# A transformer layer's experts with their weights copied into a new layout beside attention, and used as the stationary side of the first product

## The chip, the cores and the metric

The kernel runs on one core of a Trainium2 chip, as one launch. The metric is the time of the device in microseconds (us), the median over several runs. A profile is one more execution, recorded by the hardware profiler. The core has a matrix engine (PE, with a weight load, PEld, ahead of each matmul), a vector engine (DVE), a scalar engine for activations (ACT), GpSimd (POOL), and SyncE (SP), which mostly issues transfers. Sixteen DMA engines move data between the DRAM and the on-chip SBUF; PSUM is the on-chip memory of eight banks that PE writes its results into.

## The reference

Two layers on 4096 tokens (2 x 2048) of 512 features, all in float32. The first is a linear attention, the second a mixture of experts; each is normalised before and after and added to its input.

```python
x = x + _layernorm(_L0_attn_ref(_layernorm(x), Wq, bq, Wk, bk, Wv, bv, Wo))
x = x + _layernorm(_L0_ffn_ref(_layernorm(x), wg, w1, v1, w2))

# attention: 16 heads of 128, 4 key/value heads
sq, sk = elu(q) + 1, elu(k) + 1
kv = einsum('bhsd,bhse->bhde', sk, v)
attn = einsum('bhsd,bhde->bhse', sq, kv) / (einsum('bhsd,bhd->bhs', sq, sk.sum(axis=2))[..., None] + EPS)

# experts: 32 of them, 8 per token, F = 192 hidden features
weights, idx = top_k(softmax(x @ wg.T), 8); weights = weights / weights.sum()
h  = silu(ragged_dot(xs, w1, group_sizes)) * ragged_dot(xs, v1, group_sizes)   # xs: tokens sorted by expert
ys = ragged_dot(h, w2, group_sizes)
out = zeros.at[t_s].add(ys * w_s[:, None])
```

## The kernel before

**Attention.** `keys_of` normalises and transposes all tiles of one of the two sequences and forms the keys' state; `finish_kv` and `fold_wo` turn it into one matrix per head. Then four blocks of 512 tokens for each sequence, eight in all, go through `attn_block`. It walks over 16 heads: `stage_q(h)` forms the head's queries on PE (L552, eight instruction records: four chunks of 128 input features, two records per float32 matmul), ACT takes Relu and Exp (L555, L556) and DVE forms `sq` (L559). After every fourth head `stage_n` forms the normalisers on PE (L567), DVE takes the reciprocal (L571), and they go through DRAM: SP writes `nr_d` (L573) and loads it back four times, spread over all partitions, as `nb` (L576), with which DVE multiplies `sq` (L579). Eight heads later `stage_o` multiplies with the head's matrix (L584). While a block runs, the four tiles of 128 tokens of the block before are finished (`finish_tile`): added to the input, normalised, written to `xn_d`, and routed. `route_tile` finds the eight experts of each token and scatters token numbers and weights into a list per expert, with eight indirect DMAs per tile on POOL (L203). In the first block SP also clears the accumulators in DRAM (`acc_d`, L429).

**Experts.** The lists are cut into blocks of 128 tokens of one expert each; two halves of them ("sides", s = 0 and 1) are worked on in pairs. 138 pairs run: 24 in a first round, planned from the first six attention blocks, and 114 in a second one, of which the last ten stand behind conditions (`tc.If`) that ask whether there are still pairs to do. For one pair:

- `prepare`: for each side SP reads the expert's number from the plan and loads its weights into one of NR = 3 buffers: `w1t` (L674, [128, 4 x 384]: for each of the four chunks of 128 input features the 192 gate and then the 192 up columns) and `w2t` in two pieces of 128 and 64 rows (L675, L676). A load is skipped where the buffer still holds that expert. POOL gathers the 128 tokens from `xn_d` (L679), PE transposes them in four pieces (`px`, L685), DVE copies them to `xgT` (L687).
- `run_pair`: for each side PE forms `pgu` = tokens x weights (L698): the tokens' transposes are stationary, 384 weight columns move, four chunks, thus eight records; the result has tokens in the partitions and 384 features along the row. ACT takes SiLU of the 192 gate columns (`hs`, L701) and DVE multiplies by the 192 up columns into `hh` (L702), with the features put in an order in which the two sides' 2 x 192 make three pieces of 128. PE transposes the three pieces (`ph`, L710), DVE copies them (`hT`, L712). The second product (`py`, L715 for the first 128 features of a side, L719 for the other 64) gives 512 columns per side; ACT scales by the token's weight (`ysb`, L723) and POOL adds the rows into `acc_d` by an indirect DMA (L724).

PSUM is full in this stage: two banks each for `xt`, `gu` and `y`, one for `ht`, one for the routing.

A scheduler orders the instructions on each engine after the whole program is written; on SP the order inside the expert stage is that of the program text. `tc.issue_after(ins)` keeps what is written under it behind `ins` on that engine. At the end `acc_d` is read back, normalised, added and written out (L767 to L789).

Of the kernel before, what the change touches and what calls it, by code (L numbers as in the profile page):

```python
# [8 lines left out]
F32 = mybir.dt.float32  # L9
I32 = mybir.dt.int32  # L10
U32 = mybir.dt.uint32
AF = mybir.ActivationFunctionType
# [5 lines left out]
P = 128  # L18
# [5 lines left out]
def linear_attention_then_moe(  # L24
# [15 lines left out]
    nc = tc.nc  # L40

    NT, HID = x.shape
    B = 2
# [5 lines left out]
    C = HID // P  # L49
    E = wgT.shape[1]  # L50
    K = 8
    F2 = wgu.shape[1] // C
    F = F2 // 2
    FC = w2r.shape[1] // HID
    FR = F - P
# [4 lines left out]
    NBLK = S // TB  # L60
# [20 lines left out]
    dram = ctx.enter_context(tc.tile_pool(name="dram", bufs=1, space=DRAM))  # L81
# [4 lines left out]

    nr_d = dram.tile([B * NBLK, KVH, GR * TB], F32, name="nr_d")
    list_d = dram.tile([E * CAP + BS, 2], F32, name="list_d")


    const = ctx.enter_context(tc.tile_pool(name="const", bufs=1))
    ident = const.tile([P, P], F32, name="ident")
# [284 lines left out]
    with ExitStack() as actx:  # L377
# [153 lines left out]
        def fold_wo(acc):  # L531
# [9 lines left out]
                ms.append(m)  # L541
            return ms

        def attn_block(b, t, xlT, ksum, ms):

            pa = [ps_acc.tile([P, HID], F32, tag="acc", name=f"acc{s}") for s in range(NS)]
            sq, sqn = {}, {}

            def stage_q(h):
                pq = ps_mm.tile([P, TB], F32, tag="mm", name="pq")  # L550
                for c in range(C):
                    nc.tensor.matmul(pq, wq_sb[:, c, h * P : (h + 1) * P], xlT[:, c, :],  # L552
                                     start=(c == 0), stop=(c == C - 1))
                qe = wk2.tile([P, TB], F32, tag="qe", name="qe")
                nc.scalar.activation(qe, pq, AF.Relu, bias=nbq_sb[:, h : h + 1], scale=-1.0)  # L555
                ex = nc.scalar.activation(qe, qe, AF.Exp, scale=-1.0)  # L556

                sq[h] = sqp.tile([P, TB], F32, tag="sq", name="sq")
                nc.vector.scalar_tensor_tensor(sq[h], pq, bq1_sb[:, h : h + 1], qe, ALU.add, ALU.max)  # L559
                return ex.ins  # L560

            def stage_n(g):

                pn = ps_mm.tile([P, TB], F32, tag="mm", name="pn")
                w = P // GR
                for j in range(GR):
                    nc.tensor.matmul(pn[j * w : (j + 1) * w, :], ksum[:, g, 1, :w], sq[g * GR + j],  # L567
                                     start=True, stop=True)
                nr = wk2.tile([P, TB], F32, tag="tmp", name="nr")
                nc.vector.tensor_scalar_add(nr, pn, NORM_EPS)  # L570
                nc.vector.reciprocal(nr, nr)  # L571
                rows = nr_d[b * NBLK + t, g : g + 1, :]
                nc.sync.dma_start(rows.rearrange("o (j f) -> (o j) f", j=GR), nr[::w, :])  # L573
                for j in range(GR):
                    nb = nbp.tile([P, TB], F32, tag="nb", name="nb")
                    nc.sync.dma_start(nb, rows[:, j * TB : (j + 1) * TB].to_broadcast([P, TB]))  # L576
                    h = g * GR + j
                    sqn[h] = sq.pop(h)
                    nc.vector.tensor_mul(sqn[h], sqn[h], nb)  # L579

            def stage_o(h):
                a = sqn.pop(h)
                for s in range(NS):
                    nc.tensor.matmul(pa[s], a[:, s * P : (s + 1) * P], ms[h],  # L584
                                     start=(h == 0), stop=(h == H - 1))

            for h in range(H + 2 * GR):
                if h < H:
                    ex = stage_q(h)
                if h == H // 2:  # L590
                    mid = ex
                if h < H and h % GR == GR - 1:
                    stage_n(h // GR)
                if h >= 2 * GR:
                    stage_o(h - 2 * GR)
                if h % GR == GR - 1:
                    finish_next()

            for s in range(NS):
                mv, rs = ln_stats(sm, pa[s])  # L600
                x1 = x1p.tile([P, HID], F32, tag="x1", name="x1")
                nc.vector.tensor_scalar(x1, pa[s], mv[:, 0:1], rs, ALU.subtract, ALU.mult)
                waiting.append(((b * S + t * TB) // P + s, x1))
            return mid
# [42 lines left out]
    with ExitStack() as mctx:  # L647
# [5 lines left out]
        hp = pairs.enter_context(tc.tile_pool(name="hp", bufs=3))  # L653
        ps_a = pairs.enter_context(tc.tile_pool(name="ps_a", bufs=2, space=PSUM))
# [4 lines left out]

        w1b = weights([P, C * F2], "w1t")  # L660
        w2b = weights([P, 2, HID], "w2t")

        w2v = w2r.rearrange("r (c h) -> (r c) h", c=FC)
        pairs.enter_context(tc.manual_schedule(engines={mybir.EngineType.SP}))

        def prepare(r, cols, tid, wt, load, xsrc):

            xgTs = []
            for s, c0 in enumerate(cols):
                w1t, w2t = w1b[s][r], w2b[s][r]  # L670
                ld = nc.sync.value_load(load[:, c0 : c0 + 1], min_val=0, max_val=2 * E - 1)
                ex = ld & (E - 1)
                skip = {"cond": ld < E, "bounds_check": "skip_entire_dma"}
                nc.sync.dma_start(w1t, wgu[bass.ds(ex * P, P), :], **skip)  # L674
                nc.sync.dma_start(w2t[:, 0, :], w2v[bass.ds(ex * F + s * FR, P), :], **skip)  # L675
                nc.sync.dma_start(w2t[s * FR : (s + 1) * FR, 1, :],  # L676
                                  w2v[bass.ds(ex * F + (1 - s) * P, FR), :], **skip)
                xg = xg_p.tile([P, HID], F32, tag="xg", name="xg")
                nc.gpsimd.indirect_dma_start(  # L679
                    out=xg, out_offset=None, in_=xsrc,  # L680
# [9 lines left out]

        def run_pair(r, cols, tid, wt, load, xgTs):

            hh = hp.tile([P, 2, F], F32, tag="hh", name="hh")
            for s, xgT in enumerate(xgTs):
                w1t = w1b[s][r]
                pgu = ps_a.tile([P, F2], F32, tag="gu", name="pgu")
                for c in range(C):
                    nc.tensor.matmul(pgu, xgT[:, c, :], w1t[:, c * F2 : (c + 1) * F2],  # L698
                                     start=(c == 0), stop=(c == C - 1))
                hs = hp.tile([P, F], F32, tag="hs", name="hs")  # L700
                nc.scalar.activation(hs, pgu[:, :F], AF.Silu)  # L701
                nc.vector.tensor_mul(  # L702
                    hh[:, s, :].rearrange("p (k c) -> p c k", c=FC),
                    hs.rearrange("p (c k) -> p c k", c=FC),
                    pgu[:, F:].rearrange("p (c k) -> p c k", c=FC),
                )
            hf = hh.rearrange("p s f -> p (s f)")
            ph = ps_a.tile([P, 3, P], F32, tag="ht", name="ph", bufs=1)
            for c in range(3):
                nc.tensor.transpose(ph[:, c, :], hf[:, c * P : (c + 1) * P], ident)  # L710
            hT = hp.tile([P, 3, P], F32, tag="hT", name="hT")
            nc.vector.tensor_copy(hT, ph)  # L712
            py = [ps_a.tile([P, HID], F32, tag="y", name=f"py{s}") for s in range(2)]
            for s in range(2):
                nc.tensor.matmul(py[s], hT[:, 2 * s, :], w2b[s][r][:, 0, :],  # L715
# [114 lines left out]
```

## Time and profile before

| | |
|---|---|
| Median of 3 runs | 2855.16 us (2854.49 to 2856.72) |
| The profiled execution | 2861.29 us, span of its instructions 2859.5 us |
| PE busy | 2645.8 us, 93% of the span, 8443 records |
| DVE, ACT, POOL busy | 37%, 24%, 37% |
| pgu (L698) | 2208 records, 780.0 us busy |
| ph (L710) | 414 records, 100.5 us busy |
| px (L685) | 1104 records, 174.2 us busy |
| hh (L702), hT (L712) | 276 of 355 ns, 138 of 557 ns |
| w1t loads (L674) | 276 issues of 768 KB, a part of them skipped |
| DMA | 399.83 MB, 140 GB/s on average |

A line of the profile names the source line, the engine, the operation, what it writes and reads, and the shapes; "x" is the number of records. Ends of matmuls are modelled and overlap the next one's start, so the time of a run of matmuls is read from start to start. The "idle before" of an instruction names what ended the wait. From the start to about 150 us come the first sequence's keys, then its four attention blocks to about 660, the second sequence's keys to about 820 and its blocks to 1335; the experts follow to 2775, the last normalisation to 2859.

### The profile page before, as it was taken

How to read it: one execution, taken by the hardware profiler on the slowest of the kernel's cores; microseconds unless marked ns; L12 is line 12 of the kernel's file. 1: busy time of each engine (PE TensorE's matmuls, PEld its weight loads, DVE VectorE, ACT ScalarE, POOL GpSimd, SP SyncE). 2: the span in 40 equal slices, each digit the busy share in tenths (PEclk: the TensorE clock that was granted, in tenths of full speed). 3: DMA queues.
4: the chain of work that ended last, by engine and by line, in shares of the span. 5: the costliest groups of instructions: out<-in, count | busy, mean ns of one | idle time of the engine just before them, and what ended most of it. 6: DMA issues, size and time to landing. Idle time of an engine off the chain costs nothing. (4 is left out here: it accounts for less than half of the span.)

```text
span 2859.5 us, 29618 instructions
## 1 busy us (share of the span) xinstructions
PE 2645.8 (93%) x8443; PEld 1310.7 (46%) x8443; DVE 1061.4 (37%) x2432; ACT 674.8 (24%) x1208; POOL 1059.9 (37%) x891
## 2 busy tenths in 40 slices
PE   8999999998999999998779899999999999999850
PEld 3434444444444444444435455555555555555420
DVE  5334544546533536554412222222222222222217
ACT  4332222213331313221211112121212121212114
POOL 1100223122320122223455555555555555554426
PEclk9999999999999999999889999999999999999985
DMA  3291211212111212123647899989787988685548
GB/s 112 86 329 51 68 52 52 68 52 67 37 56 45 71 34 71 53 71 114 161 102 175 212 268 257 274 200 254 165 214 160 314 194 199 137 194 114 104 87 323
DMA packets 179290, 399.83 MB, mean 140 GB/s; under 512 B 29413, under 2 KB 30438, under 8 KB 178610
## 3 DMA queue, kind: packets, MB, share of 16 engines
q0 software_dynamic: 70144, 145.31, 25.1%
q1 hardware_dynamic: 101602, 237.55, 24.9%
q10 hardware_dynamic: 7376, 15.02, 1.4%
q8 instruction: 70, 1.15, 0.2%
q14 instruction: 98, 0.80, 0.1%
HBM read 488.74 MB, written 116.66 MB: 212 GB/s over the span
## 5 line engine op out<-in xcount | busy, mean ns | idle before, releaser
L698 PE MATMUL pgu<-w1t,xgT 128*128 128x384 f32 x2208 | 780.0, 496 | 3.5 <-issue 2.4
L724 POOL DMA_INDIRECT acc_d<-ysb,tid x276 | 441.9, 1601 | 503.8 <-ACT ysb L723 389.5
L203 POOL DMA_INDIRECT list_d<-tw,pi x256 | 252.2, 985 | 979.6 <-DVE pi L201 556.2
L698 PEld LDWEIGHTS pgu<-w1t,xgT 128*128 128x128 f32 x2208 | 399.5, 191 | 327.2 <-issue 109.3
L552 PE MATMUL pq<-xlT,wq_sb 128*128 128x512 f32 x1024 | 463.1, 598 | 1.2 <-DVE sq L559 1.2
L584 PE MATMUL acc<-m,sq 128*128 128x512 f32 x1024 | 463.0, 597 | 0.0
L702 DVE TENSOR_TENSOR hh<-hs,pgu 128x192 f32<-128x192 f32 x276 | 97.3, 355 | 975.9 <-ACT hs L701 838.2
L723 ACT ACTIVATE ysb<-py,wt 128x512 f32<-128x512 f32 x276 | 176.5, 684 | 783.4 <-PE py L719 731.8
L679 POOL DMA_INDIRECT xg<-xn_d,tid x276 | 274.9, 996 | 119.0 <-PE px L685 64.0
L552 PEld LDWEIGHTS pq<-xlT,wq_sb 128*128 128x128 f32 x1024 | 190.7, 190 | 241.5 <-issue 230.8
L584 PEld LDWEIGHTS acc<-m,sq 128*128 128x128 f32 x1024 | 189.1, 190 | 239.6 <-issue 239.1
L715 PE MATMUL py<-w2t,hT 128*128 128x512 f32 x552 | 266.4, 605 | 2.1 <-issue 2.1
L555 ACT ACTIVATE qe<-pq,nbq_sb 128x512 f32<-128x512 f32 x128 | 87.8, 686 | 514.6 <-PE pq L552 509.0
L687 DVE COPY xgT<-px 128x512 f32<-128x512 f32 x276 | 188.3, 683 | 43.6 <-PE px L685 41.3
L559 DVE SCALAR_TENSOR_TENSOR sq<-pq,bq_sb,qe 128x512 f32<-128x512 f32 x128 | 95.8, 748 | 286.0 <-ACT qe L556 285.9
L685 PE MATMUL px<-ident,xg 128*128 128x128 f32 x1104 | 174.2, 284 | 29.1 <-DMA xg<-xn_d,tid 26.7
L701 ACT ACTIVATE hs<-pgu 128x192 f32<-128x192 f32 x276 | 90.3, 330 | 363.2 <-PE pgu L698 336.7
L685 PEld LDWEIGHTS px<-ident,xg 128*128 128x128 f32 x1104 | 135.9, 147 | 56.9 <-issue 32.0
L715 PEld LDWEIGHTS py<-w2t,hT 128*128 128x128 f32 x552 | 107.5, 196 | 109.2 <-issue 74.0
L719 PE MATMUL py<-w2t,hT 64*128 64x512 f32 x552 | 157.1, 642 | 0.0
L710 PE MATMUL ph<-ident,hh 128*128 128x128 f32 x414 | 100.5, 298 | 51.3 <-DVE hh L702 51.2
L469 PE MATMUL pk<-wk_sb,xlT 128*128 128x512 f32 x256 | 119.7, 607 | 0.0
(185 smaller groups left out, 1844.8 us busy)
## 6 DMA issues: line engine op xcount, KB each, us to landing
w1t<-in_wgu_dram SPq DMA_DIRECT2D x276, 768.0 KB
w2t<-in_w2r_dram SPq DMA_DIRECT2D x276, 256.0 KB
w2t<-in_w2r_dram SPq DMA_DIRECT2D x276, 128.0 KB
nb<-nr_d SPq DMA_DIRECT2D x128, 256.0 KB
acc_d<-zero SPq DMA_DIRECT2D x6, 2048.0 KB
xb<-in_x_dram SPq DMA_DIRECT2D x32, 256.0 KB
xr<-in_x_dram SPq DMA_DIRECT2D x32, 256.0 KB
wo<-in_woT_dram SPq DMA_DIRECT2D x32, 256.0 KB
```

The source lines that it names most:

```text
L203: nc.gpsimd.indirect_dma_start(out=list_d[:, :], out_offset=bass.IndirectOffsetOnAxis(ap=pi[:, k : k + 1], axis=0), in_=tw[:, k, :], in_of ...
L469: nc.tensor.matmul(pk, xlT[:, c, :], wk_sb[:, c, :], start=(c == 0), stop=(c == C - 1))
L552: nc.tensor.matmul(pq, wq_sb[:, c, h * P : (h + 1) * P], xlT[:, c, :], start=(c == 0), stop=(c == C - 1))
L584: nc.tensor.matmul(pa[s], a[:, s * P : (s + 1) * P], ms[h], start=(h == 0), stop=(h == H - 1))
L679: nc.gpsimd.indirect_dma_start(out=xg, out_offset=None, in_=xsrc, in_offset=bass.IndirectOffsetOnAxis(ap=tid[:, c0 : c0 + 1], axis=0),)
L685: nc.tensor.transpose(px[:, c, :], xg[:, c * P : (c + 1) * P], ident)
L687: nc.vector.tensor_copy(xgT, px)
L698: nc.tensor.matmul(pgu, xgT[:, c, :], w1t[:, c * F2 : (c + 1) * F2], start=(c == 0), stop=(c == C - 1))
L715: nc.tensor.matmul(py[s], hT[:, 2 * s, :], w2b[s][r][:, 0, :], start=True, stop=False)
L719: mm = nc.tensor.matmul(py[s], hT[rows, 1, :], w2b[s][r][rows, 1, :], start=False, stop=True)
L723: nc.scalar.activation(ysb, py[s], AF.Copy, scale=wt[:, c0 : c0 + 1])
L724: sc = nc.gpsimd.indirect_dma_start(out=acc_d[s][:, :], out_offset=bass.IndirectOffsetOnAxis(ap=tid[:, c0 : c0 + 1], axis=0), in_=ysb, in_ ...
```

## The change

Two new tensors in DRAM, `w1_d` and `w2_d`, hold the experts' weights in a new order: for each chunk of input features the 384 columns stand as the 192 gate columns (0 to 191), then the last 64 up columns (192 to 255), then the first 128 up columns (256 to 383). Read in three strips of 128: gate 0 to 127; gate 128 to 191 with up 128 to 191; up 0 to 127. `w2_d` has the 192 rows of an expert in their plain order.

`lay_out_experts(i)` yields five copies from DRAM to DRAM for four experts: three for `w1_d` (pieces of 768, 256 and 512 bytes) and two for `w2_d` (rows of 2 KB). `attn_block` issues them on ACT's queue after the Exp of heads 1, 4, 7, 10 and 13; with eight blocks this covers the 32 experts with 40 copies, 37.7 MB read and as much written.

`prepare` loads from `w1_d` and `w2_d`. In `run_pair` the weights are now the stationary side: for each side three strips by four chunks, each a matmul of a 128x128 piece of weights with the 128 tokens moving. The result has features in the partitions and tokens along the row, as the second product needs it, so the three transposes and the copy to `hT` are gone. ACT takes SiLU over the first two strips (256 columns), and DVE forms `hT` with two products, one of 128 partitions and one of 64, the latter with operands from different partitions. `pgu` has three buffers, and the bank of `ph` is free for the third.

```diff
--- before.py
+++ after.py
@@ -86,6 +86,10 @@
 
     nr_d = dram.tile([B * NBLK, KVH, GR * TB], F32, name="nr_d")
     list_d = dram.tile([E * CAP + BS, 2], F32, name="list_d")
+
+
+    w1_d = dram.tile([E * P, C * F2], F32, name="w1_d")
+    w2_d = dram.tile([E * F, HID], F32, name="w2_d")
 
 
     const = ctx.enter_context(tc.tile_pool(name="const", bufs=1))
@@ -541,10 +545,26 @@
                 ms.append(m)
             return ms
 
+        def lay_out_experts(i):
+
+            n = E // (B * NBLK)
+            rows = slice(i * n * P, (i + 1) * n * P)
+            src = wgu[rows, :].rearrange("r (c f) -> r c f", c=C)
+            dst = w1_d[rows, :].rearrange("r (c f) -> r c f", c=C)
+            yield lambda: nc.scalar.dma_start(dst[:, :, :F], src[:, :, :F])
+            yield lambda: nc.scalar.dma_start(dst[:, :, F : F + FR], src[:, :, F + P :])
+            yield lambda: nc.scalar.dma_start(dst[:, :, F + FR :], src[:, :, F : F + P])
+            w2s = w2r[i * n * (F // FC) : (i + 1) * n * (F // FC), :]
+            w2x = w2_d[i * n * F : (i + 1) * n * F, :].rearrange("(e c p) h -> c e p h", e=n, c=FC)
+            for c in range(FC):
+                yield lambda c=c: nc.scalar.dma_start(
+                    w2x[c], w2s[:, c * HID : (c + 1) * HID].rearrange("(e p) h -> e p h", e=n))
+
         def attn_block(b, t, xlT, ksum, ms):
 
             pa = [ps_acc.tile([P, HID], F32, tag="acc", name=f"acc{s}") for s in range(NS)]
             sq, sqn = {}, {}
+            moves = lay_out_experts(b * NBLK + t)
 
             def stage_q(h):
                 pq = ps_mm.tile([P, TB], F32, tag="mm", name="pq")
@@ -587,6 +607,9 @@
             for h in range(H + 2 * GR):
                 if h < H:
                     ex = stage_q(h)
+                    if h % 3 == 1 and h < 15:
+                        with tc.issue_after(ex):
+                            next(moves)()
                 if h == H // 2:
                     mid = ex
                 if h < H and h % GR == GR - 1:
@@ -659,8 +682,6 @@
 
         w1b = weights([P, C * F2], "w1t")
         w2b = weights([P, 2, HID], "w2t")
-
-        w2v = w2r.rearrange("r (c h) -> (r c) h", c=FC)
         pairs.enter_context(tc.manual_schedule(engines={mybir.EngineType.SP}))
 
         def prepare(r, cols, tid, wt, load, xsrc):
@@ -671,10 +692,10 @@
                 ld = nc.sync.value_load(load[:, c0 : c0 + 1], min_val=0, max_val=2 * E - 1)
                 ex = ld & (E - 1)
                 skip = {"cond": ld < E, "bounds_check": "skip_entire_dma"}
-                nc.sync.dma_start(w1t, wgu[bass.ds(ex * P, P), :], **skip)
-                nc.sync.dma_start(w2t[:, 0, :], w2v[bass.ds(ex * F + s * FR, P), :], **skip)
-                nc.sync.dma_start(w2t[s * FR : (s + 1) * FR, 1, :],
-                                  w2v[bass.ds(ex * F + (1 - s) * P, FR), :], **skip)
+                nc.sync.dma_start(w1t, w1_d[bass.ds(ex * P, P), :], **skip)
+                nc.sync.dma_start(w2t[:, 0, :], w2_d[bass.ds(ex * F, P), :], **skip)
+                nc.sync.dma_start(w2t[s * FR : (s + 1) * FR, 1, :], w2_d[bass.ds(ex * F + P, FR), :],
+                                  **skip)
                 xg = xg_p.tile([P, HID], F32, tag="xg", name="xg")
                 nc.gpsimd.indirect_dma_start(
                     out=xg, out_offset=None, in_=xsrc,
@@ -690,26 +711,20 @@
 
         def run_pair(r, cols, tid, wt, load, xgTs):
 
-            hh = hp.tile([P, 2, F], F32, tag="hh", name="hh")
+
+            hT = hp.tile([P, 3, P], F32, tag="hT", name="hT")
             for s, xgT in enumerate(xgTs):
-                w1t = w1b[s][r]
-                pgu = ps_a.tile([P, F2], F32, tag="gu", name="pgu")
-                for c in range(C):
-                    nc.tensor.matmul(pgu, xgT[:, c, :], w1t[:, c * F2 : (c + 1) * F2],
-                                     start=(c == 0), stop=(c == C - 1))
-                hs = hp.tile([P, F], F32, tag="hs", name="hs")
-                nc.scalar.activation(hs, pgu[:, :F], AF.Silu)
-                nc.vector.tensor_mul(
-                    hh[:, s, :].rearrange("p (k c) -> p c k", c=FC),
-                    hs.rearrange("p (c k) -> p c k", c=FC),
-                    pgu[:, F:].rearrange("p (c k) -> p c k", c=FC),
-                )
-            hf = hh.rearrange("p s f -> p (s f)")
-            ph = ps_a.tile([P, 3, P], F32, tag="ht", name="ph", bufs=1)
-            for c in range(3):
-                nc.tensor.transpose(ph[:, c, :], hf[:, c * P : (c + 1) * P], ident)
-            hT = hp.tile([P, 3, P], F32, tag="hT", name="hT")
-            nc.vector.tensor_copy(hT, ph)
+
+                pgu = ps_a.tile([P, 3, P], F32, tag="gu", name="pgu", bufs=3)
+                w1t = w1b[s][r].rearrange("p (c k f) -> p c k f", c=C, k=3)
+                for k in range(3):
+                    for c in range(C):
+                        nc.tensor.matmul(pgu[:, k, :], w1t[:, c, k, :], xgT[:, c, :],
+                                         start=(c == 0), stop=(c == C - 1))
+                hs = hp.tile([P, 2, P], F32, tag="hs", name="hs")
+                nc.scalar.activation(hs, pgu[:, :2, :], AF.Silu)
+                nc.vector.tensor_mul(hT[:, 2 * s, :], hs[:, 0, :], pgu[:, 2, :])
+                nc.vector.tensor_mul(hT[s * FR : (s + 1) * FR, 1, :], hs[:FR, 1, :], pgu[FR:, 1, :])
             py = [ps_a.tile([P, HID], F32, tag="y", name=f"py{s}") for s in range(2)]
             for s in range(2):
                 nc.tensor.matmul(py[s], hT[:, 2 * s, :], w2b[s][r][:, 0, :],
```

## The prediction

> **What bounds the kernel now.** I read the page first for the engines' shares, then stretches of the span, then the order on the matmul engine inside one stretch. Busy time by stretch: the first row is attention, the second the steady part of the expert stage (columns: length, then busy us of each engine, granted clock, DMA share, GB/s).
>
> ```profile
> core 0: us, PE busy (x) PEld busy (x) DVE busy (x) ACT busy (x) POOL busy (x), PEclk, DMA share, GB/s
> 150.00:1335.00 1185.00, 1159.25 (x3159) 510.90 (x3157) 573.66 (x1326) 308.48 (x504) 240.29 (x241) 0.99 0.21 70
> 1600.00:2634.00 1034.00, 1032.46 (x3809) 560.40 (x3806) 261.67 (x549) 209.49 (x435) 561.62 (x432) 1.00 0.84 213
> ```
>
> PE is without a gap in the expert stage (1032.46 of 1034.00) and 98% busy in attention, at full clock; DVE, ACT and POOL stand at half or less. DMA is lightly used in attention (0.21) and heavily in the expert stage (0.84). So an expert pair lasts as long as its PE instructions. One pair on PE, in order of time (start, us, what, count):
>
> ```profile
> 2009.27 1.88 PE L715 MATMUL py<-w2t,hT 128*128 128x512 f32 x4
> 2011.08 1.13 PE L719 MATMUL py<-w2t,hT 64*128 64x512 f32 x4
> 2012.13 4.14 PE L698 MATMUL pgu<-w1t,xgT 128*128 128x384 f32 x12
> 2016.11 0.27 PE L710 MATMUL ph<-ident,hh 128*128 128x128 f32 x1
> 2016.22 0.93 PE L685 MATMUL px<-ident,xg 128*128 128x128 f32 x7
> 2017.08 0.44 PE L710 MATMUL ph<-ident,hh 128*128 128x128 f32 x2
> 2017.36 0.27 PE L685 MATMUL px<-ident,xg 128*128 128x128 f32 x1
> 2017.47 1.46 PE L698 MATMUL pgu<-w1t,xgT 128*128 128x384 f32 x4
> 2018.76 0.59 PE L715 MATMUL py<-w2t,hT 128*128 128x512 f32 x1
> ```
>
> From start to start, because ends overlap: the pair lasts 2018.76 - 2009.27 = 9.49 us. The first product has 16 records (two per matmul in float32): 2012.13 to 2016.11 and 2017.47 to 2018.76, together 3.98 + 1.29 = 5.27 us, 0.325 to 0.332 each. The three feature transposes take 0.11 + 0.28 = 0.39, and the seven px records take 0.86 where their own pace (0.93 less the last one's 0.273, over six gaps) is 0.1095, that is 0.77; the other 0.09 is PE waiting for hh. So the transposes cost 0.48 us a pair.
>
> **The first product after the change.** Weights become stationary: for each block 3 strips of 128 features by 4 chunks by two records, 24 records of 128x128 instead of 8 of 128x384; 48 a pair instead of 16, each with its own weight load. Nearest rows: the two products of 128x128 float32 that attention already has, one weight load to each record.
>
> ```profile
> 804.07 1.05 PE L519 MATMUL pc<-ones,sks 128*128 128x128 f32 x8
> 804.96 3.89 PE L525 MATMUL pg<-gc,wv_sb 128*128 128x128 f32 x32
> 808.69 1.88 PE L538 MATMUL pm<-wo,kvacc 128*128 128x512 f32 x4
> ```
>
> L519: (1.05 - 0.275)/7 = 0.1107 us from record to record. L525: (3.89 - 0.275)/31 = 0.1166 over all, but its readers on DVE (L527) start at 806.18, 807.11, 808.00 and 808.89, thus 0.93, 0.89 and 0.89 for eight records, 0.113 once it runs; the second strip had to wait for a PSUM copy that ended at 805.85. I take 0.113, with ends 0.1107 and 0.1166: 48 x 0.113 = 5.42 us (5.31 to 5.60), 0.15 more than now.[...]
>
> Net on PE: -0.48 + 0.15 = -0.33 us a pair.
>
> **The way from the first product to the second.** Removed: ph and the copy hT (DVE, 0.557). In their place: SiLU over 256 columns instead of 192 (0.330 at 192 and 0.684 at 512, so 0.40), and two DVE products of 128 columns (0.355 at 192, 0.683 at 512 for a copy; 0.29 each). From the end of the product to hT: 0.40 + 0.58 + three hand-overs of 0.05 to 0.2 = 1.3 us. PE has to fill this with other work: px (8 x 0.11 = 0.88) and the next pair's first strips (pgu has three buffers now, up to 24 x 0.113 = 2.7). Where the order puts enough of them ahead of py, the cost is nothing; where it puts only px, a hole of 0.4 us. I take 0.05. DVE falls from 1.27 to 1.16 a pair, ACT rises by 0.14: both hidden under PE.
>
> **How many pairs.** 1034 / 9.49 = 109 in the steady stretch, six of the eight between 2658 and 2740, about three before 1600: 118 of 138. The others (1335 to 1600) wait for POOL's list scatter, not for PE. (-0.33 + 0.05) x 118 = -33 us. At the three or four places where a part ends and nothing fills, the way from SiLU to py is 1.91 us (2733.63 to 2735.54) and becomes some 1.3: -2 us.
>
> **The loads of the expert stage** keep their size, pieces and order on SP; they read w1_d and w2_d. The first is issued at 1335.09, after the last attention matmul; the last copy is issued behind the exponential of head 13 of the last block, near 1287, and ends by 1310 at its upper cost: no wait. The 3% faster pace raises the DMA share from 0.84 to 0.87; stretches of 305 GB/s pass today with PE full.
>
> **The copies beside attention.** 40 DMAs from DRAM to DRAM, five to a block, at heads 1, 4, 7, 10, 13, on ACT's queue. ACT issues a DMA in 0.34 (L440) to 0.38 us (L789), 0.69 for one of many pieces (L439): 40 x 0.4 = 16 us (up to 28), in gaps of 2.1 us or more between heads: nothing. SP shows one issue of 5.0 us (L429[...]); on ACT that would make the next head 2.9 us late, which the second PSUM buffer covers (3.43 us of matmuls): 0, at worst a few us.
> No row shows such a copy. Pieces: three w1 copies of 2048 (768, 256 and 512 bytes), 128 per DMA engine; two w2 copies of 384 pieces of 2 KB. From the queues (packets, MB, share of 16 engines)
>
> ```profile
> q1 hardware_dynamic: 101602, 237.55, 24.9%
> q10 hardware_dynamic: 7376, 15.02, 1.4%
> ```
>
> a packet takes share x 16 x 2859.5 / packets = 0.112 and 0.087 us. A w1 copy is then 11 to 14 us (below: 1.4 us for the 0.5 MB one by bytes at the 368 GB/s that the clearing at 150 to 175 reaches).[...]
> Who meets them: the four nb loads of each group, on the critical side of DVE:
>
> ```profile
> 865.27 1.74 SPq L576 DMA_DIRECT2D nb<-nr_d  x4
> 868.67 1.33 DVE L579 TENSOR_TENSOR sq<-sq,nb 128x512 f32<-128x512 f32 x2 [3.49 <-DMA nb<-nr_d]
> ```
>
> They land after 3.4 us, and DVE stands waiting at its head; behind it are the next head's sq, and behind that pn and the PSUM buffer of pq on PE. If each of nb's 8 packets per engine lets one copy packet pass, one nb is 0.7 to 0.9 us later and four 2.8 to 3.6; DVE's own gap of 2.7 us between heads takes most of it. 32 groups: 0 to 115 us, I take 0.25 each, +8 us. The list scatter on POOL (2.38 us each, 32 to a block, 76 of 125 us) may grow by 0.9 each to 105: still hidden; beyond 125 DVE would wait for tw.
>
> **Sum.** -33 - 2 + 8 = -27 us. The profiled execution took 2861.29 us (span 2859.5 and 1.8 around it); the median shown is 2855.16, 6 us lower, and I set the difference against the median: **2828 us**.
>
> **Rivals.**
> A, the gain as summed: 2828, own range 2800 (0.1107 a record, no hole, no contention: 2855 - 0.44 x 118 - 2 = 2801) to 2849. Chance 0.62.
> B, the gain is lost to a hole before py of 0.3 to 0.4 us a pair, or to ACT, POOL or DMA that cannot follow (DVE hh waited for ACT's ysb 87.7 us in this stretch, without PE waiting): 2828 + 0.3 x 118 = 2863, or no change. Against: PE waited 1.3 us there in all. 0.14.
> C, the small records run as pl (L152, 31.8 us for 256, 0.124): 48 x 0.124 = 5.95, +0.20 a pair, +0.05 of hole, + 6: 2890. It decides from 0.118 a record. Against: pl's figure holds the start of each short run. 0.10.
> D, **slower than before**: contention in attention. The copies make each of 32 nb groups late on DVE, in front of PE; at 2 us each 64 us instead of 8: 2884. It decides from (27 + 8)/32 = 1.1 us a group. For: PE is 98% busy there, so a stall is lost time, and DVE already waits 3.49 us at one place. Against: DMA is idle for 80% of it. 0.14.
>
> **Numbers.** 0.2% (6 us) is what a measurement of this kernel can tell from no change: 2849.4 to 2860.9. Faster: A, 0.63 with B's edge. Same: B's half and A's and D's edges, 0.12. Slower: C, D and half of B, 0.25. The range reaches over B and into C and D: 2800 to 2868.
>
> **What would show it.** Right: no L710; about 48 pgu records a pair at 0.111 to 0.115 and a pair of 9.15 to 9.25 us; attention's stretch within 10 us of 1185. Wrong: records at 0.118 or more; PE waiting for hT ahead of py; DVE L579 waiting for nb in most groups, or POOL's list scatter taking over 3 us; an ACT issue of several us.

## The result and the profile after

The changed kernel takes **3007.73 us** (median, 3000.25 to 3012.73) where the kernel before takes 2854.9; the ratio is 1.0532, with a 95% interval of 1.0519 to 1.0545 (intervals below are of the same kind). It is 5.3% slower, 180 us above the forecast and well outside its range.

Where the time went is seen by cutting the span at the first load of an expert's weights, right behind the last product of attention. Before, it is issued at 1335.1 us; after, at 1489.6: **154.5 us lost in attention**. From there to the end the spans have 1524.4 and 1514.6 us: 9.8 us won by the experts. Attention before and then after, and 200 us of the changed expert stage (columns: length, busy us of PE, PEld, DVE, ACT and POOL with their records, granted clock of PE as a share of full speed, DMA share, GB/s):

```profile
0.00:1335.10 1335.10, 1295.63 (x3543) 575.55 (x3543) 637.88 (x1468) 367.11 (x586) 262.25 (x272) 0.99 0.23 74
```

```profile
0.00:1489.60 1489.60, 1331.74 (x3543) 584.40 (x3543) 633.16 (x1461) 383.48 (x597) 261.33 (x271) 0.95 0.29 92
1900.00:2100.00 200.00, 199.73 (x1352) 149.48 (x1350) 51.96 (x128) 43.56 (x85) 110.65 (x86) 1.00 0.91 243
```

PE has the same 3543 records in both attention rows. It stands idle for 1489.6 - 1331.7 = 157.9 us in place of 39.5, which is 118 us, and the same records are busy 36 us longer, at a granted clock of 0.95 in place of 0.99. DMA is still lightly used (0.29). In the expert stage (last row) PE is full, as it was.

Who stands idle for what, in the waits of the whole changed kernel:

```profile
engine line waited for: us in total, times, longest us
POOL list_d L207 <- DMA list_d<-tw,pi: 469.7, 214, 7.4
DVE tw L183 <- DMA list_d<-tw,pi: 302.8, 28, 17.6
PE pn L587 <- DVE sq L579: 85.7, 28, 8.0
DVE sq L599 <- DMA nb<-nr_d: 63.8, 44, 4.7
```

The wait of DVE that grew most is not the one the forecast feared. Its wait for `nb` is 63.8 us (20.9 before). Its wait to write `tw`, the pairs of token number and weight for the lists, is 302.8 (53.3 before). Nearly all of those 53.3 us lay in attention, where this row stood:

```profile
DVE tw L179 <- DMA list_d<-tw,pi: 51.3, 12, 17.7
```

One such wait in the changed kernel, in order of time: first DVE, then PE, then the stretches around it (columns as above):

```profile
387.81 0.19 DVE L158 TENSOR_REDUCE nmx<-pl 128x1 f32<-128x32 f32 x1 [1.17 <-PE pl L156]
403.79 0.17 DVE L183 COPY tw<-tok 128x8 f32<-128x8 f32 x1 [15.79 <-DMA list_d<-tw,pi]
403.87 1.40 DVE L579 SCALAR_TENSOR_TENSOR sq<-pq,bq_sb,qe 128x512 f32<-128x512 f32 x2
```

```profile
394.56 6.17 PE L604 MATMUL acc<-m,sq 128*128 128x512 f32 x14
404.67 2.57 PE L587 MATMUL pn<-sq,kvacc 128*32 128x512 f32 x8 [3.94 <-DVE sq L579]
```

```profile
400.00:404.67 4.67, 0.73 (x2) 0.00 (x0) 0.88 (x3) 0.00 (x0) 0.96 (x1) 1.00 0.01 0
404.67:407.30 2.63, 2.63 (x9) 0.46 (x9) 2.31 (x15) 0.00 (x0) 0.00 (x0) 0.60 0.00 0
407.30:411.00 3.70, 3.70 (x8) 2.15 (x9) 3.40 (x3) 0.00 (x0) 0.00 (x0) 0.50 0.00 0
411.00:415.00 4.00, 4.00 (x9) 1.75 (x9) 1.69 (x5) 1.24 (x2) 0.96 (x1) 0.87 0.11 24
```

L183 copies a constant column (the tile's token numbers) into `tw`. It stands at the head of DVE's queue for 15.79 us until a list scatter has landed; the two `sq` behind it are ready to run (ACT's part of them ended at 387.24), and go 0.08 us after it starts. PE wants them for `pn` and has nothing else in its order: 3.94 us idle. Then it pays a second time: the eight `pn` records take 2.57 us, where at full clock eight took 1.07 (at 262.45), at a granted clock of 0.60, then 0.50, and 0.87 up to 415.

Shorter gaps of the same trace were followed by a low clock in one place and not in another. These are the stretches behind a gap of 2.46 us (ended at 345.45) and behind one of 2.37 us (ended at 367.76):

```profile
345.45:349.00 3.55, 3.55 (x12) 1.39 (x13) 0.00 (x0) 0.00 (x0) 0.35 (x1) 1.00 0.16 53
367.76:371.00 3.24, 3.23 (x4) 0.97 (x5) 1.63 (x8) 0.00 (x0) 0.00 (x0) 0.50 0.00 0
```

So the length of a gap alone does not tell here what the clock will do. In sum the clock can account for the 36 us of longer busy time. In attention the granted clock is 0.50 in 17 stretches of the changed kernel, with PE busy for 92.6 us of their 146.8; before, it is so in four, with 14.7 us busy of 17.1. Six `pn` records took 1.93 us in such a stretch (444.23) and 1.06 at full clock (169.47). If half of the 77.9 us more is lost time, an estimate from these figures, that is 39 us, where 36 were measured.

One expert pair after, on PE, and the way of the second side from the first product to the second:

```profile
2107.60 2.13 PE L730 MATMUL py<-w2t,hT 128*128 128x512 f32 x4
2109.66 1.13 PE L734 MATMUL py<-w2t,hT 64*128 64x512 f32 x4
2110.72 1.09 PE L706 MATMUL px<-ident,xg 128*128 128x128 f32 x8
2111.65 5.52 PE L722 MATMUL pgu<-xgT,w1t 128*128 128x128 f32 x48
2117.01 2.13 PE L730 MATMUL py<-w2t,hT 128*128 128x512 f32 x4
```

```profile
2107.85 0.38 ACT L725 ACTIVATE hs<-pgu 128x256 f32<-128x256 f32 x1 [2.35 <-PE pgu L722]
2108.26 0.29 DVE L726 TENSOR_TENSOR hT<-hs,pgu 128x128 f32<-128x128 f32 x1 [2.12 <-ACT hs L725]
```

The 48 `pgu` records take 2117.01 - 2111.65 = 5.36 us, 0.1117 each; `ph` is gone. But `py` follows `pgu` at once, and its four records take 2.06 us from start to start in place of 1.81: the second side's `hT` comes at 2108.55, in the middle of them. The pair takes 9.41 us, only 0.08 less than before.

### The profile page after: what moved, and what is told of

It is laid out like the page before. It is cut to its first block, busy times and chain, and to the rows that moved or that the text cites. A ratio compares the mean times of both kernels' runs of the same rounds, so it can differ in the third digit from the quotient of the medians.

```text
span 3004.2 us, 38001 instructions
## 1 busy us (share of the span) xinstructions
PE 2678.4 (89%) x12445; PEld 1589.5 (53%) x12445; DVE 1062.5 (35%) x2570; ACT 711.6 (24%) x1224; POOL 1053.3 (35%) x891
## 3 DMA queue, kind: packets, MB, share of 16 engines
q10 hardware_dynamic: 63120, 52.77, 5.6%
## 5 line engine op out<-in xcount | busy, mean ns | idle before, releaser
L722 PE MATMUL pgu<-xgT,w1t 128*128 128x128 f32 x6624 | 772.9, 277 | 6.0 <-DVE xgT L708 5.5
L722 PEld LDWEIGHTS pgu<-xgT,w1t 128*128 128x128 f32 x6624 | 757.6, 193 | 16.0 <-DVE xgT L708 10.5
L572 PE MATMUL pq<-xlT,wq_sb 128*128 128x512 f32 x1024 | 481.3, 619 | 5.4 <-DVE sq L579 5.4
L730 PE MATMUL py<-w2t,hT 128*128 128x512 f32 x552 | 303.1, 637 | 34.2 <-DVE hT L726 32.7
L726 DVE TENSOR_TENSOR hT<-hs,pgu 128x128 f32<-128x128 f32 x276 | 79.4, 288 | 623.4 <-ACT hs L725 577.1
L725 ACT ACTIVATE hs<-pgu 128x256 f32<-128x256 f32 x276 | 105.5, 384 | 666.1 <-PE pgu L722 495.5
L706 PEld LDWEIGHTS px<-ident,xg 128*128 128x128 f32 x1104 | 123.0, 145 | 144.3 <-issue 120.6
L706 PE MATMUL px<-ident,xg 128*128 128x128 f32 x1104 | 157.3, 286 | 37.9 <-DMA xg<-xn_d,tid 24.8
L734 PE MATMUL py<-w2t,hT 64*128 64x512 f32 x552 | 164.3, 657 | 0.0
L730 PEld LDWEIGHTS py<-w2t,hT 128*128 128x128 f32 x552 | 85.3, 194 | 146.3 <-DVE hT L726 107.7
L587 PE MATMUL pn<-sq,kvacc 128*32 128x512 f32 x256 | 77.3, 715 | 85.7 <-DVE sq L579 85.7
```

The lines of the kernel that those rows point to most:

```text
L706: nc.tensor.transpose(px[:, c, :], xg[:, c * P : (c + 1) * P], ident)
L722: nc.tensor.matmul(pgu[:, k, :], w1t[:, c, k, :], xgT[:, c, :], start=(c == 0), stop=(c == C - 1))
L734: mm = nc.tensor.matmul(py[s], hT[rows, 1, :], w2b[s][r][rows, 1, :], start=False, stop=True)
```

## The experiments

All ratios are taken against the kernel before on the same chip, 2852 to 2854 us.

### The two halves of the change apart

The copies alone, put ahead of the old experts, which go on reading `wgu` and `w2r`:

```diff
+            moves = lay_out_experts(b * NBLK + t)
...
+                    if h % 3 == 1 and h < 15:
+                        with tc.issue_after(ex):
+                            next(moves)()
```

> The kernel before with the 40 copies at the same places in attention and nothing else: its experts still read the old layout, the copies' result is not used. On every engine its order in attention is that of the changed kernel. Both theories put the loss into attention: about 145 to 155 us over before, thus 2995 to 3015. If the loss were in the experts (small records, loads from the new tensors), 2855 to 2865.

Measured: 3008.28 us, ratio 1.0546 (1.0528 to 1.0564). The first expert product starts at 1498.2. The copies alone lose all that the change loses (153 us).

The experts alone: the changed kernel without copies, the loads taken from the old tensors. The columns then stand in another order than the products assume, so other features are multiplied with each other; the instructions and bytes are those of the changed experts.

```diff
-                    if h % 3 == 1 and h < 15:
-                        with tc.issue_after(ex):
-                            next(moves)()
...
-                nc.sync.dma_start(w1t, w1_d[bass.ds(ex * P, P), :], **skip)
+                nc.sync.dma_start(w1t, wgu[bass.ds(ex * P, P), :], **skip)
```

> The changed kernel without its copies; the experts load from the inputs in the old column order with the same shapes, so gate and up columns are mixed up and the sum is another one, the work the same. Attention has before's order. By the prediction's steps 2820; by the changed kernel's trace, where PE waits 0.25 us a pair for hT between the two sides' second products and the pair takes 9.41 instead of 9.49 us, 2842 to 2848.

Measured: 2844.59 us, 0.9967 (0.9956 to 0.9978): -9.4 us where the sum had -35. The halves add up to 154 - 9 = 145 us, and together they lose 153; the other 8 us were not explained.

### Bytes, or the order of the instructions

The copies are part of the program that the scheduler orders. In the built kernels the order in attention differs between before and after on PE, DVE, ACT and SP; the kernel with the copies alone has the changed kernel's order there. So two more kernels. In the first, every copy is issued under a condition that is never true: the order of the kernel with the copies, and no bytes. (The traces agree: PE's 3543, DVE's and ACT's instructions up to the first expert follow one another in the same sequence in both.)

```diff
+        nv = nc.scalar.value_load(never_t[:1, :1], min_val=0, max_val=7)
+        never = {"cond": nv < 1, "bounds_check": "skip_entire_dma"}
...
-            yield lambda: nc.scalar.dma_start(dst[:, :, :F], src[:, :, :F])
+            yield lambda: nc.scalar.dma_start(dst[:, :, :F], src[:, :, :F], **never)
```

> As the copies alone, but each copy stands under a condition that is false at run time, so no byte moves; the order of the instructions on PE, DVE, ACT, POOL and SP is that of the run with the copies. Theory 'order' (the scheduler plans for long copies and lays attention's instructions out anew): nearly the same loss, 2970 to 3010. Theory 'traffic' (copies in flight delay nb and the list scatter): the loss is gone, 2855 to 2870.

Measured: 2916.12 us, 1.0208 (1.0181 to 1.0235). **62 us come without a byte moved.** DVE's wait for `tw` in attention is 158 us.

In the second, the same bytes go in 128 copies of one expert each (`w2_d` in one copy, over 96 rows), one after each head. That leaves nearly the order of before: 5226 of PE's 5265 instructions keep their places.

```diff
-            rows = slice(i * n * P, (i + 1) * n * P)
-            src = wgu[rows, :].rearrange("r (c f) -> r c f", c=C)
+            for e in range(i * n, (i + 1) * n):
+                src = wgu[e * P : (e + 1) * P, :].rearrange("r (c f) -> r c f", c=C)
...
-                    if h % 3 == 1 and h < 15:
-                        with tc.issue_after(ex):
-                            next(moves)()
+                    with tc.issue_after(ex):
+                        next(moves)()
```

> The kernel before with the same bytes copied, as 128 smaller copies (one after each head, a quarter of the size, w2 over 96 rows[...]) instead of 40. Attention's order on PE is then nearly that of before (5226 of 5265 instructions in the same sequence). 'Order': 2855 to 2880. 'Traffic': the same bytes beside attention, so a loss like that of the 40 copies, 2950 to 3010.

Measured: 2913.59 us, 1.0204 (1.0187 to 1.0221). So the bytes cost 60 us in nearly the old order and 92 (3008 - 2916) in the new one.

The bytes by kind, in the order of the kernel with the copies: only those for `w1_d`, or only those for `w2_d`, with the condition above on the others. (The expectation's megabytes are four times too high; the copies move 25.2 and 12.6 MB. Its sums use only the share of two thirds.)

> The order of the kernel with the copies alone, in which only the 24 copies of w1 move bytes (100 MB of 151); the 16 copies of w2 are under a condition that is never true. Order alone is +62 us, all copies +154. If the cost of the traffic goes with the bytes, this one is 2854 + 62 + 61 = 2977 us.[...]

> The mirror of it: the 16 copies of w2 move bytes (50 MB), the 24 of w1 do not. By bytes: 2854 + 62 + 31 = 2947 us.[...]

Measured: 2947.72 us (1.0329, 1.0312 to 1.0347) and 2947.31 us (the same ratio). Each adds 31 to 32 us to the order's 62, where together they add 92. The cost does not go with the bytes: `w2_d`, with a third of them, costs as much as `w1_d`. Which transfer slows which was not traced further, because the next runs made it matter little.

### The write of tw

Its wait is for a scatter that still reads the buffer: three buffers, four tiles to a block. First, more buffers, seven for `tw` and `pi` (two in place of three for `mk` and `pos`, to make room):

```diff
-        tw = sm.tile([P, K, 2], F32, tag="tw", name="tw")
+        tw = sm.tile([P, K, 2], F32, tag="tw", name="tw", bufs=7)
...
-        pi = sm.tile([P, K], I32, tag="pi", name="pi")
+        pi = sm.tile([P, K], I32, tag="pi", name="pi", bufs=7)
```

> The forty copies ahead of the old experts, in the same order of instructions as in the kernel with the copies alone (3008 us, 154 above before), but with seven buffers in place of three for tw and for the positions pi, so that VectorE's write of tw no longer has to wait until the list scatter of three tiles earlier has landed. Theory 1, VectorE stands behind the scatters, and everything queued behind it (sq, then pn, then nr) with it: the wait of tw, 255 us in attention, falls under 30 us and the time falls to 2870 to 2920 us. Theory 2, what costs is the broadcast nb and the other transfers on SP's queue, tw is a wait that would be taken elsewhere: the tw wait goes, but waits for nb or for PE grow in its place and the time stays at 2980 to 3010 us. Theory 3, POOL itself is backed up by slow scatters: the time falls by less than 40 us and the routing ends late, with the first expert load after the last attention product.

> The same seven buffers for tw and pi in the kernel whose copies are issued under a condition that is never true (no bytes move; 2916 us, of which 62 us come from the order alone). Theory 1, the new order hurts because it puts the write of tw nearer to the scatters of the tile before: 2855 to 2875 us. Theory 2, the new order hurts in itself, on PE and ACT (px, pq, qe following one another in another sequence): the time stays at 2905 to 2920 us.

Measured: 2994.32 us (1.0495, 1.0474 to 1.0515) with the copies, 2906.62 (1.0191, 1.0172 to 1.021) with those that move nothing: 14 and 10 us. The first run's wait, in attention:

```profile
DVE tw L181 <- DMA list_d<-tw,pi: 251.4, 23, 18.4
```

Theory 1 as written there said this wait would fall under 30 us, and it did not move (255 us with three buffers). The 14 us fit theory 3, slow scatters that back up POOL itself; the tied kernel below, in which POOL waits for them as long, speaks against it. The order of the built kernels says why the wait stayed. The copy of the token column needs nothing from its tile; the scheduler puts it as far forward as a buffer is free. With three buffers three such copies stand ahead of the first routed tile, with seven buffers seven; from then on both kernels have them at nearly the same places, each just behind the scatters that free a buffer. More buffers only make the copy belong to a later tile.

So the copy itself has to be held back. It is tied, by `tc.issue_after`, to come behind the reciprocal of the tile's own sum:

```diff
-        nc.vector.reciprocal(tsum, tsum)
+        rc = nc.vector.reciprocal(tsum, tsum)
         tw = sm.tile([P, K, 2], F32, tag="tw", name="tw")
-        nc.vector.tensor_copy(tw[:, :, 0], tok[:, i : i + 1].to_broadcast([P, K]))
+        with tc.issue_after(rc.ins):
+            nc.vector.tensor_copy(tw[:, :, 0], tok[:, i : i + 1].to_broadcast([P, K]))
```

> The forty copies ahead of the old experts (3008 us), with the write of the token number tied in the same way; 5243 of PE's 5265 instructions keep their places in the order, SP's and POOL's all. The wait of that write was 255 us in attention, and seven buffers did not change it (251 us), since the write moves ahead by as many tiles as there are buffers. Theory 1, the write at the head of VectorE's queue is what the copies' order and slow scatters cost: the time falls to 2870 to 2920 us. Theory 2, the broadcast nb and transfers on SP's queue cost it: the tw wait goes, the time stays at 2970 to 3010 us.

> The same tie where the copies' condition is never true (2916 us, tw wait 158 us). Theory 1: 2850 to 2875 us. Theory 2, PE's and ACT's new sequence costs it: 2900 to 2920 us.

> The kernel before, no copies, with one line held back: VectorE's write of the token number into tw, which needs nothing of the tile and so may be put anywhere once its buffer is free, is tied to come after the reciprocal of the tile's own sum of weights. In attention it waited 51 us for list scatters. Theory 1, this write stands at the head of VectorE's queue until scatters land: the wait goes; 2830 to 2850 us. Theory 2, its wait was time in which VectorE had nothing better to do: 2850 to 2858 us.

| | as it was | write tied | first expert product starts at, untied and tied |
|---|---|---|---|
| kernel before | 2852.85 | 2846.44 (0.9977, 0.9966 to 0.9988) | 1344.4, 1338.2 |
| copies that move nothing | 2916.12 | 2892.71 (1.0142, 1.0125 to 1.0159) | 1406.0, 1383.9 |
| copies, old experts | 3008.28 | 2905.86 (1.0189, 1.0172 to 1.0206) | 1498.2, 1397.7 |

One line held back gives 102 us with the copies, 23 without their bytes, 6 without copies. (The untied kernels with copies ran on another chip than the tied ones; the kernel before took 2854.0 there, which moves these differences by about 1 us.) In the kernel with the copies, in attention, first untied and then tied:

```profile
POOL list_d L205 <- DMA list_d<-tw,pi: 362.0, 164, 6.5
DVE tw L181 <- DMA list_d<-tw,pi: 255.0, 23, 18.4
PE pn L585 <- DVE sq L577: 80.1, 22, 8.0
```

```profile
POOL list_d L206 <- DMA list_d<-tw,pi: 400.7, 179, 7.4
DVE nr L589 <- PE pn L586: 199.4, 31, 17.2
PE pn L586 <- DVE sq L578: 22.8, 12, 3.2
DVE tw L182 <- DMA list_d<-tw,pi: 0.2, 1, 0.2
```

The scatters are as slow as before the tie (POOL waits 400.7 us for them here, 362.0 in the untied kernel), but DVE no longer stands behind them, and PE's wait for `sq` falls from 80.1 to 22.8. The tied kernels differ by 13 us with and without the bytes. That is what the traffic costs once DVE no longer waits for a scatter.

Theory 1 had 2850 to 2875 us for the kernel whose copies move nothing, and it is at 2893: 46 us above the tied kernel before. Two runs asked whether these belong to the order, and whether the changed kernel is the same case:

> Small copies, the same bytes in 128 pieces one after each head's exponential, in an order of attention that is nearly that of the kernel before (5226 of 5265 on PE), old experts, with the tie. Without the tie 2914 us. Theory 1, after the tie only the scheduler's new order was left to pay for: 2850 to 2865 us. Theory 2, the issuing on ACT's queue (138 copies at about 0.6 us) and the traffic keep costing: 2895 to 2910 us.

> The changed kernel whole, with nothing altered but the tie of the token write. The same tie took 102 us from the kernel with the copies alone (2906 us), and the new experts are worth 9 us: 2890 to 2905 us if the loss of the changed kernel is that of its copies; over 2950 us if the changed kernel loses in another way too.

Measured: the small copies, in nearly the old order, **2857.46 us** (1.0014, 1.0008 to 1.0021), 56 less than untied and 11 above the tied kernel before, with 37.7 MB relaid in full. (They are 128, not 138, copies.) The changed kernel, tied: 2897.68 (1.0156, 1.0134 to 1.0177), 110 less. The 128 issues on ACT's queue and all bytes cost 11 us at most in the old order, so by elimination the 46 us are the order's. Both tied kernels of the new order, with and without bytes, have DVE at `nr` waiting for PE's `pn` 199 us, up to 17.2 at once, where the small copies have

```profile
DVE nr L587 <- PE pn L584: 44.1, 32, 2.1
```

This points to `nr` being placed too early on DVE, with other work behind it; it was not tested alone.

### The hole between the two products

Without copies, three strips can be cut from a row of `wgu` as it is: gates 0 to 191 and ups 0 to 191 follow one another, so columns 128 to 255 are gates 128 to 191 with ups 0 to 63. It takes three products on DVE a side and three loads of `w2t`. `prepare` and `run_pair` were split, so that the next pair's transposes are written between the two products:

```diff
+                nc.vector.tensor_mul(hT[:FR, 2 * s, :], hs[:FR, 0, :], pgu[FR:, 1, :])
+                nc.vector.tensor_mul(hT[FR:, 2 * s, :], hs[FR:, 0, :], pgu[:FR, 2, :])
+                nc.vector.tensor_mul(hT[s * FR : (s + 1) * FR, 1, :], hs[:FR, 1, :], pgu[FR:, 2, :])
...
+                xgs = prepare(*pair2(i + 1), xn_d[:, :]) if i + 1 < i0 + n else []
+                hT = first(*pair2(i), ready)
+                ready = turn_tokens(xgs)
+                second(hT, *pair2(i))
```

> No copies. The experts' weights are read where they are: in a row of w1 the gates 0 to 191 and the ups 0 to 191 are already one after another, so three strips of 128 columns are cut without a new layout (gate 0-127; gate 128-191 with up 0-63; up 64-191), at three products on VectorE a side in place of two and three w2 loads a side in place of two; and the next pair's turning of its tokens (px, 8 transposes) is put on PE between the first and the second products, where PE otherwise waits some 0.25 us for hT. Theory 1, the first product costs 5.4 us and the hole closes: a pair takes 9.49 - 0.33 = 9.16 us, 118 pairs, 2854 - 39 = 2815 us. Theory 2, the hole only moves (VectorE's six products a pair are late, or px waits for its token rows): 2840 to 2850 us.

Measured: 3100.15 us, 1.0861 (1.0843 to 1.0879), 247 slower than before; neither theory had that. PE in its steady stretch:

```profile
2111.01 1.10 PE L723 MATMUL py<-w2t,hT 128*128 128x512 f32 x2
2111.94 2.84 PE L710 MATMUL pgu<-xgT,w1t 128*128 128x128 f32 x24
2114.71 1.12 PE L727 MATMUL py<-w2t,hT 64*128 64x512 f32 x2
2115.77 0.66 PE L694 MATMUL px<-ident,xg 128*128 128x128 f32 x4
2116.26 1.07 PE L723 MATMUL py<-w2t,hT 128*128 128x512 f32 x2
2117.26 1.12 PE L727 MATMUL py<-w2t,hT 64*128 64x512 f32 x2
```

The scheduler took the two sides apart, and two 64-row records now take what four took when they stood together (1.13 us, L734 above). One side's rows are partitions 0 to 63, the other's 64 to 127. In the changed kernel, where they stand together, the first two of the four at L734 both start by 2109.67 and last 0.69 us each. Parted, they cost 1.06 us more a pair, some 125 us over 118 pairs. A second part of the 247 stands in this kernel's waits: PE's transposes `px` now wait for DVE's copy `xgT` of the ones before.

```profile
PE px L694 <- DVE xgT L696: 79.2, 124, 0.8
```

Some 40 us are left unexplained.

With PE's order of the expert stage written out (and the write of `tw` tied):

```diff
-        pairs.enter_context(tc.manual_schedule(engines={mybir.EngineType.SP}))
+        pairs.enter_context(tc.manual_schedule(engines={mybir.EngineType.SP, mybir.EngineType.PE}))
```

> No copies; three strips of 128 columns cut from w1's rows as they are, w2 in three loads a side, the tie of the token write, and PE's order of the expert stage written out: 48 records of the first product, 8 transposes of the next pair's tokens, 4 second products of 128 rows, 4 of 64 rows side by side. Theory 1, nothing waits between the products: a pair takes 5.36 + 0.93 + 1.81 + 1.06 = 9.16 us in place of 9.49, 118 pairs, 2846 - 39 = 2807 us (to 2815 with the ends). Theory 2, the six narrow products of VectorE a pair hold hT up behind the two copies of px: 2835 to 2850 us. In the run that let the scheduler order PE (3100 us) two 64-row records took 1.12 us where four took 1.13 before; if parting them was the loss there, they must be back at 1.13 us for four here.

Measured: 2843.13 us, 0.9964 (0.9948 to 0.9979), with

```profile
2106.26 5.62 PE L711 MATMUL pgu<-xgT,w1t 128*128 128x128 f32 x48
2111.72 1.04 PE L695 MATMUL px<-ident,xg 128*128 128x128 f32 x8
2112.59 1.88 PE L724 MATMUL py<-w2t,hT 128*128 128x512 f32 x4
2114.41 1.13 PE L728 MATMUL py<-w2t,hT 64*128 64x512 f32 x4
2115.46 5.62 PE L711 MATMUL pgu<-xgT,w1t 128*128 128x128 f32 x48
```

The four 64-row records are back at 1.13, `py` at 1.82, and the pair takes 9.20 us. Yet the kernel is only 3 us below the tied kernel before. In the first round, which was written out without the next pair's transposes between, PE's `py` waits for `hs` up to 7.4 us at once. Two kernels test whether that was the loss:

> The kernel without copies as in the run before, with PE's order written out in the second round alone; the first round's 24 pairs are the scheduler's. If the first round was the loss: 2843 - 24 to 34, so 2810 to 2822 us. If the scheduler takes apart the first round's 64-row pairs, as in the run with the reordered emission (1.1 us a pair), or the loss is one of loads arriving late (DMA share 0.96 to 0.98 there), 2835 to 2850 us.

> The same with PE's order written out in both rounds, and in the first too with the next pair's transposes between the products. If the unfilled waits of the first round were the loss: 2810 to 2822 us. If it is loads and gathers that arrive late: 2835 to 2850 us.

Measured: 2842.22 us (0.9962, 0.9948 to 0.9976) with the first round left to the scheduler, which parted its 64-row pairs again, and **2833.18 us** (0.9931, 0.9917 to 0.9945) with both rounds written out. The second is the fastest kernel here, 20 us below before and 13 below the tied kernel before, but short of the 2810 to 2822 forecast. At the change of rounds its `px` waits once for gathered rows:

```profile
1650.11 1.11 PE L695 MATMUL px<-ident,xg 128*128 128x128 f32 x4 [9.75 <-DMA xg<-xn_d,tid]
```

and in the first round `py` still waits for `hs` four times, 3.9 to 5.6 us each, between 1440 and 1500. Over the expert stage this wait is 22.8 us, where it was 22.7 before the transposes were put between: the cover did not shorten it. In the profiles the first 24 pairs take 312.8 us, from the first product of the first to that of the 25th; they took 327.0 without the cover and 304.2 in the tied kernel before. So the first round still loses 9 us to the old kernel. Why, and where the rest of the forecast gain went, stays open.

## Why the prediction was wrong

**The copies beside attention** is the step that failed: +8 us, and they cost 154. Its parts:

- *The order.* The step costed the copies in an attention that otherwise stays as it was, and said nothing of the scheduler. 62 us came with no bytes; 46 of them stay when the write of `tw` is tied.
- *Who meets the copies.* The step, and rival D with it, put the meeting at the `nb` loads, and passed over the scatters: "beyond 125 DVE would wait for tw", as if DVE waited only when POOL is a whole block behind. The write stands behind a scatter as soon as that has not landed, and the trace of before showed it doing so for 51.3 us. Of the 155 us of the copies alone (3008.28 - 2852.85), 96 go with this one write (102 less the 6 that its tie gives without copies), 46 with the order, 13 with all other traffic. The waits for `nb`, which the step counted, grew too, from 20.9 to 63.8 us; the 0.25 us that it took for each group of four loads was the author's estimate.
- *What an idle PE costs.* The step counted a stall at its length. Beside 118 us of idle time there were 36 of longer busy time, at a granted clock of 0.50.
- *The price of a packet* was 0.087 to 0.112 us. From the queue's rows it is (0.056 x 16 x 3004.2 - 0.014 x 16 x 2859.5) / (63120 - 7376) = 0.037. The copies were cheaper than assumed, and still the loss came. ACT's issues took 0.52 to 0.67 us, not 0.4; with the tie and the old order they and the traffic are within 11 us.

```profile
q10 hardware_dynamic: 63120, 52.77, 5.6%
```

Rival D named the right side and the right place, at 2884 us and 0.14, by another wait.

**The first product** held: 48 records at 0.1117 us (0.113 taken), 5.36 us a pair (5.42). `ph` with its 0.48 us went. `hs` took 0.384 us (0.40), a product for `hT` 0.288 (0.29).

**The way from the first product to the second** was mis-sized: 0.05 us a pair taken, 0.25 measured, inside its bounds of 0 to 0.4. The order has `px` ahead of `pgu` and nothing between `pgu` and `py`. The eight `px` took 0.93 us, where 0.88 was counted, the rest of the difference. So a pair gained 0.08 us and not 0.28, and 118 x 0.08 = 9.4 us is what the experts alone measured. Where the hole was filled, the pair took 9.20, within 0.01 of the forecast's 9.21.

**The loads of the expert stage** were not late. DMA's share rose to 0.91 there with PE still full.

## What to carry to other kernels

Before adding work beside a stage that fills one engine, list the waits of the engines that feed it. Here the scheduler moved an instruction that needs nothing of its own tile forward until it stood behind the transfer that frees its buffer, and everything behind it on that engine waited too. Tying it to its own tile took 102 us away; more buffers took 14. And compare the order of the instructions before comparing times: a kernel with the same instructions under a condition that is never true prices the order alone.

## What the runs showed of the hardware

- A gap of 3.94 us on PE was followed by a granted clock of 0.60 and 0.50 for 6.3 us and 0.87 for four more: the eight records behind it took 1.5 us longer than at full clock. Behind a gap of 2.37 us the clock was 0.50, behind one of 2.46 us it was 1.00. Over attention PE was idle 118 us more and busy 36 us longer.
- Two 64-row float32 products on different halves of the partitions took 1.13 us for four records when they stood next to each other, and 1.12 us for two when they were apart.
- Copies from DRAM to DRAM of 256 bytes to 2 KB took 0.037 us of a DMA engine per packet, beside 0.112 in the queue of the loads, and still slowed the small scatters: in the same order of attention, POOL's mean wait for one was 309.1 / 177 = 1.75 us where no bytes moved and 362.0 / 164 = 2.21 us where they did.
